# Two attention layers on one core: the output products of step 7 placed behind the value products, with the next scores after them

## The chip, the cores and the metric

The kernel runs on one core of a Trainium2 chip. The metric is the device time in microseconds: 3507.43 us before the change, the median of three runs (3504.42 to 3509.01). The profiled execution has a span of 3507.0 us, and the mean granted TensorE clock in it is 0.998.

## The reference

Four images of 32 x 32 positions with 768 channels pass through two layers. Each layer normalizes in 32 groups of channels, computes attention with 12 heads of 64 channels over the 1024 positions of the image, with a bias for relative height and width, projects the result, and adds it to its input. Cut to what matters:

```python
for Wq, Wk, Wv, Wproj, bproj, Rh, Rw in layers:      # layer 1 also has biases for q, k, v and scales twice
    n = group_norm(x)                                # 32 groups
    q, k, v = n @ Wq, n @ Wk, n @ Wv                 # 12 heads of 64
    s = scale * q @ k.T + (q @ Rh)[..., :, None] + (q @ Rw)[..., None, :]
    x = x + (softmax(s) @ v) @ Wproj + bproj
```

Everything is in float32.

## The kernel before

Activations lie with the channels on the 128 partitions and the 1024 positions (S) along the free axis. Two layers by four images make 8 image passes, run one after the other. Heads are worked in pairs: a pair is 128 channels, one head in partitions 0 to 63 and one in 64 to 127, six pairs (NP) to an image, 48 pairs (NPAIR) in all, counted by g. Each pair has 8 steps (NT), counted by n; a step is 128 query positions against all 1024 key positions, for both heads. The main loop at L566 goes through these 384 units (g, n) in order.

The order of the instructions is written out by hand: the block at L542 fixes it for all engines, and each engine runs its own instructions in the order in which the code issues them. The tile pools still add the waits for data and buffers. In one turn of the loop, unit (g, n), the code issues, in this order:

- run(early) at L595: what earlier steps left to be done, such as stores, loads of weights, the position products (L281) and the statistics for the next normalization (L152).
- biases (L319, GpSimd): the bias tile of the unit two ahead, 128 x 1024 for each head, into the pool sc.
- scores (L333) of the unit one ahead: eight TensorE instructions in four calls, into the PSUM pool ps_s, which has two buffers, one for each head. VectorE then adds the bias and finds the row extreme in one pass from PSUM to SBUF (L342, one for each head); this is what frees the PSUM buffer. ScalarE takes the exponential with the row sum (L346).
- run(behind) at L601: DMA reads that bring the transposed weights back.
- turn (L370, VectorE): the 32 x 32 block transposes of the weights of the unit itself, one for each head; every second step a DMA writes them to DRAM (td) and a later one reads them back (pt), which finishes the transposition.
- divide (L353 on VectorE, L356 on GpSimd): the reciprocals of the row sums of the unit one ahead, and the product of its exponentials with them.
- take: a share of a list of TensorE work that fills the step. The list of a pair is 36 parts for the next pair's projections (q and k at L214, v at L249), then 12 parts of output products (L475). The shares are 6, 6, 0, 6, 12, 6, 0, 12 by step, so that step 7 has the 12 output parts: four groups of three calls of 128 x 128 by 128 x 512, each evicted by VectorE (L486 or L488). The projections and the output products, like the value products, use the PSUM pool ps_m with two buffers.
- weigh (L399): the value products, for the first half of the queries at the end of step 6, for the second half at the end of step 2 of the next pair.

The output products of step 7 belong to an earlier image or to the pairs before, never to the weights just computed. In the first image, pairs 0 to 2 have none: there is no image before. In pair 4, three steps and step 7 also apply the next image's normalization on VectorE (L193), one pass for each of six chunks.

In TensorE's order, the border between two pairs is therefore: value products of step 6, scores of (g+1, 0), in step 7 the twelve output parts, then in step 0 of the next pair the scores of (g+1, 1) and the first six projection parts. Line numbers here and in the profile are those of the kernel before.

## Time and profile before

| engine | busy us | share of the span |
|---|---|---|
| PE (TensorE, matmuls) | 3462.3 | 99% |
| POOL (GpSimd) | 2729.9 | 78% |
| DVE (VectorE) | 2381.1 | 68% |
| PEld (weight loads) | 1921.4 | 55% |
| ACT (ScalarE) | 1227.5 | 35% |

DMA moves 1084.54 MB at a mean of 309 GB/s; in most slices of the span the 16 engines are 80 to 90% busy.

TensorE's busy time by kind of product: q and k projections 1033.5 us, scores 750.1, value products 689.1, v projections 515.7, output products 475.8 and 33.5 (those with the last weights), positions 108.7. These overlap, since products in different halves of the array run side by side, so their sum is above the engine's own busy time.

Each row of the groups by line gives the line, engine, operation, tiles written and read, shapes and the count; then the busy time and the mean length of one in ns; then the engine's idle time just before, and what ended most of it. In a timeline a row is a merged stretch: start, length, line, tiles, count, and in brackets the idle time before it with its cause. The ends of matmuls are modelled, so on TensorE the distance between starts says more than the lengths do.

### The profile page before, as it was taken

What the parts mean: (1) busy time and instruction counts of PE and PEld (TensorE: products, weight loads), DVE (VectorE), ACT (ScalarE), POOL (GpSimd) and SP (SyncE); (2) the same over time, 40 slices, a digit from 0 to 9 for tenths busy, and PEclk for the clock granted to TensorE, in tenths of its full rate; (3) what the DMA queues carried; (4) which work ended last, traced back from release to release, by engine and by line L of the source; (5) the groups of instructions that cost most, each with busy time, mean ns of one, the idle gap of its engine ahead of it and who ended that gap; (6) DMA issues with size and microseconds to landing.
All of it is one profiled execution on the core that took longest, in us unless ns stands there. A gap on an engine that the chain in (4) does not pass through costs nothing.

```text
span 3507.0 us, 55102 instructions
## 1 busy us (share of the span) xinstructions
PE 3462.3 (99%) x21120; PEld 1921.4 (55%) x21120; DVE 2381.1 (68%) x3676; ACT 1227.5 (35%) x2040; POOL 2729.9 (78%) x1546
## 2 busy tenths in 40 slices
PE   6999999999999999999999999999999999999999
PEld 4555555555555555555555555555555555555554
DVE  4666767767677676767767667666666667666666
ACT  2334333333333333333333333333333333333331
POOL 3888887778777787788777788787787778787774
PEclk9999999999999999999999999999999999999999
DMA  4889989999899898898989989899889988898877
GB/s 137 312 308 311 332 293 337 319 316 326 304 329 323 313 316 313 312 324 305 326 305 326 320 292 332 311 331 306 300 327 324 321 298 316 319 322 295 311 275 281
DMA packets 624857, 1084.54 MB, mean 309 GB/s; under 512 B 247120, under 2 KB 310096, under 8 KB 575440
## 3 DMA queue, kind: packets, MB, share of 16 engines
q1 hardware_dynamic: 569008, 1028.29, 83.4%
q10 hardware_dynamic: 55584, 52.72, 4.4%
q8 instruction: 166, 2.72, 0.3%
q14 instruction: 99, 0.81, 0.1%
HBM read 580.59 MB, written 500.27 MB: 308 GB/s over the span
## 4 chain that ended last, share of the span: by engine, by line
PE 97%; DMA 2%; DVE 0%; SPq 0%; issue 0%; ACT 0%; POOL 0%; ACTq 0%; DVEq 0%
PE pj L214 28%; PE s L333 19%; PE av L399 19%; PE o L475 14%; PE pv L249 14%; PE tp L281 3%; DMA tdr<-t 1%; DMA pt<-td 1%; SPq L307 0%; DMA td<-tb 0%; DMA wo<-in_wo 0%; DMA xn<-in_x 0%; DVE st L152 0%; DMA rel<-tdr 0%; DMA per<-mv 0%
## 5 line engine op out<-in xcount | busy, mean ns | idle before, releaser
L319 POOL TENSOR_TENSOR sc<-rel 128x1024 f32<-128x1024 f32 x768 | 1890.4, 2485 | 38.2 <-DMA rel<-tdr 38.2
L356 POOL TENSOR_SCALAR sc<-sc,sm 128x1024 f32<-128x1024 f32 x768 | 855.1, 1127 | 686.1 <-DVE sm L353 669.2
L346 ACT ACTIVATE sc<-sc,sm 128x1024 f32<-128x1024 f32 x768 | 879.8, 1147 | 1370.9 <-DVE sm L342 1368.7
L342 DVE CUSTOM_DVE_ANT_0 sc<-s,sc 128x1024 f32<-128x1024 f32 x768 | 909.8, 1222 | 293.3 <-PE s L333 266.4
L214 PE MATMUL pj<-xn,w 64*128 64x512 f32 x4608 | 1033.5, 591 | 26.8 <-DVE xn L193 25.7
L370 DVE STREAM_TRANSPOSE tb<-sc 128x1024 f32<-128x1024 f32 x768 | 910.7, 1222 | 22.9 <-DMA td<-tb 20.5
L214 PEld LDWEIGHTS pj<-xn,w 64*128 64x128 f32 x4608 | 453.2, 188 | 568.6 <-issue 536.6
L333 PE MATMUL s<-k,q 64*128 64x512 f32 x3072 | 750.1, 598 | 7.0 <-DVE sm L342 6.9
L399 PE MATMUL av<-pt,v 128*64 128x256 f32 x6144 | 689.1, 382 | 6.1 <-DMA pt<-td 6.1
L399 PEld LDWEIGHTS av<-pt,v 128*64 128x64 f32 x6144 | 434.5, 137 | 289.8 <-ACT v L259 35.6
L249 PE MATMUL pv<-wv,xn 64*128 64x256 f32 x4608 | 515.7, 376 | 0.0
L249 PEld LDWEIGHTS pv<-wv,xn 64*128 64x128 f32 x4608 | 448.3, 187 | 90.8 <-issue 30.1
L475 PE MATMUL o<-attn,wo 128*128 128x512 f32 x1080 | 475.8, 597 | 0.2 <-DMA wo<-in_wo 0.2
L333 PEld LDWEIGHTS s<-k,q 64*128 64x128 f32 x3072 | 288.5, 187 | 299.5 <-issue 275.5
L475 PEld LDWEIGHTS o<-attn,wo 128*128 128x128 f32 x1080 | 201.4, 190 | 271.4 <-issue 260.9
L260 DVE TENSOR_TENSOR v<-pv,v 128x256 f32<-128x256 f32 x192 | 81.5, 425 | 277.6 <-ACT v L259 277.6
L259 ACT COPY v<-pv 128x256 f32<-128x256 f32 x192 | 71.5, 372 | 330.7 <-PE pv L249 282.9
L286 ACT COPY t<-tp 128x1024 f32<-128x1024 f32 x96 | 97.2, 1012 | 245.5 <-PE tp L281 148.5
L346 ACT ACTIVATION_READ_ACCUMULATOR sc<-sc,sm 128x1 f32 x768 | 143.6, 187 | 0.0
L230 DVE TENSOR_TENSOR q<-pj,q 128x512 f32<-128x512 f32 x96 | 66.4, 692 | 107.5 <-ACT q L227 56.0
L230 DVE TENSOR_TENSOR k<-pj,k 128x512 f32<-128x512 f32 x96 | 66.4, 692 | 95.5 <-ACT k L227 49.0
L281 PEld LDWEIGHTS tp<-tab,q 64*128 64x128 f32 x1536 | 100.0, 187 | 39.9 <-issue 39.6
(34 smaller groups left out, 787.6 us busy)
## 6 DMA issues: line engine op xcount, KB each, us to landing
td<-tb SPq DMA_DIRECT2D x384, 1024.0 KB, 5.9
pt<-td SPq DMA_DIRECT2D x382, 1024.0 KB, 7.6
tdr<-t ACTq DMA_DIRECT2D x96, 512.0 KB, 6.3
w<-in_wqk SPq DMA_DIRECT2D x96, 384.0 KB, 7.5
rel<-tdr SPq DMA_DIRECT2D x760, 32.0 KB, 2.3
part<-res SPq DMA_DIRECT2D x84, 256.0 KB, 5.5
res<-part SPq DMA_DIRECT2D x84, 256.0 KB, 9.1
wv<-in_wv SPq DMA_DIRECT2D x24, 768.0 KB, 8.7
```

The lines of the kernel that those rows point to most:

```text
L214: nc.tensor.matmul(t[:, a, :], lhsT=w[rows, c, :], rhs=xn[c][rows, cols], start=(c == 0), stop=(c == NC - 1),)
L230: nc.vector.tensor_tensor(to, t[1], to, ALU.add)
L249: nc.tensor.matmul(t[:, a, k, :], lhsT=xn[c][rows, (2 * i + k) * P : (2 * i + k + 1) * P], rhs=w[rows, c, :], start=(c == 0), stop=(c == N ...
L281: nc.tensor.matmul(ps[:, h, j, :], lhsT=q[rows, at * P : (at + 1) * P], rhs=tabs[l][rows, :], start=True, stop=True,)
L319: nc.gpsimd.tensor_tensor(sc.rearrange("p (a k) (u l) -> p a (k u) l", a=4, l=8), rel[:, h, 0, n, :].unsqueeze(1).unsqueeze(3).to_broadcas ...
L333: nc.tensor.matmul(ps[h][:, cols], lhsT=q[rows, n * P : (n + 1) * P], rhs=k[rows, cols], start=True, stop=True,)
L342: nc.vector.tensor_tensor_reduce(out=sc, in0=ps[h], in1=sc, scale=-scale, scalar=BIG, op0=ALU.add, op1=ALU.min, accum_out=st[:, 0, h : h + 1],
L346: nc.scalar.activation(sc, sc, AF.Exp, bias=st[:, 0, h : h + 1], scale=-1.0, accum_out=st[:, 1, h : h + 1],)
L356: nc.gpsimd.tensor_scalar(sc, sc, st[:, 2, h : h + 1], 1.0, ALU.mult, ALU.mult)
L370: nc.vector.transpose(tb[:, :, j, :], sc_of[g, n, h])
L399: nc.tensor.matmul(av[rows, at * 2 * P : (at + 1) * 2 * P], lhsT=v_of[g][:, k, rows], rhs=pt_of[g, quarter, h][:, :, k, :], start=(k == 0) ...
L475: nc.tensor.matmul(t, lhsT=wo_of[im, o, c], rhs=attn_of[im * NP + c][:, cols], start=(c == c0), stop=(c == c1 - 1),)
```

## The change

In step 7, the transposes of the unit itself and the twelve output parts move ahead of the next scores. TensorE's order at the border becomes: value products of step 6, output products, scores of (g+1, 0), scores of (g+1, 1). Value and output products both use all 128 rows of the array, scores and projections 64, so the rows change from 128 to 64 once at the border, where they changed to 64, to 128 and to 64 again before.

In the other steps, scores and run(behind) change places in the code; one issues DMA on another queue, so each engine's own order stays. In pair 4, the normalizations of chunks 3 to 5 stand one behind each of the first three groups of output products; before, two of them stood together. VectorE's order in step 7 was: L342 for both heads, first eviction, transposes, reciprocal, remaining evictions. It becomes: transposes, four evictions, L342 for both heads, reciprocal.

```diff
             if at + 2 < len(units):
                 biases(*units[at + 2])
+            run(behind)
+            behind, behind2 = behind2, behind
+            share = shares[n]
+            if n == NT - 1:
+                turn(g, n)
+                if pair == 4 and not end:
+                    for c in (3, 4, 5):
+                        take(todo, 3)
+                        share -= 3
+                        apply(c)
+                take(todo, share)
+                share = 0
             if at + 1 < len(units):
                 scores(*units[at + 1])
-            run(behind)
-            behind, behind2 = behind2, behind
             if pair == 3 and n in stages and not end:
                 stages[n]()
             if pair == 4 and n in (2, 4, 6) and not end:
                 apply(n // 2 - 1)
-            share = shares[n]
-            first = 3 if n == NT - 1 else 2 if end and pair == NP - 1 and n in (3, 4) else 0
-            first = min(first, share)
+            first = min(share, 2 if end and pair == NP - 1 and n in (3, 4) else 0)
             take(todo, first)
             share -= first
-            turn(g, n)
+            if n < NT - 1:
+                turn(g, n)
             if at + 1 < len(units):
                 divide(*units[at + 1])
-            if pair == 4 and n == 7 and not end:
-                for chunks in ((3, 4), (5,)):
-                    take(todo, 3)
-                    share -= 3
-                    for c in chunks:
-                        apply(c)
             take(todo, share)
```

## The prediction

> **What bounds the kernel now.** I began with the busy shares and the chain that ended last, then the groups by line, then the tensor engine's timeline around steps 6, 7 and 0, and last the granted clock in short windows.

> ```profile
> PE 3462.3 (99%) x21120; PEld 1921.4 (55%) x21120; DVE 2381.1 (68%) x3676; ACT 1227.5 (35%) x2040; POOL 2729.9 (78%) x1546
> PE 97%; DMA 2%; DVE 0%; SPq 0%; issue 0%; ACT 0%; POOL 0%; ACTq 0%; DVEq 0%
> L333 PE MATMUL s<-k,q 64*128 64x512 f32 x3072 | 750.1, 598 | 7.0 <-DVE sm L342 6.9
> L370 DVE STREAM_TRANSPOSE tb<-sc 128x1024 f32<-128x1024 f32 x768 | 910.7, 1222 | 22.9 <-DMA td<-tb 20.5
> L356 POOL TENSOR_SCALAR sc<-sc,sm 128x1024 f32<-128x1024 f32 x768 | 855.1, 1127 | 686.1 <-DVE sm L353 669.2
> ```

> TensorE is the chain: 97% of it, and scores wait only 6.9 us for VectorE in the whole run. VectorE and GpSimd have slack (GpSimd idles 686 us before L356). So the order of products on TensorE, and what they wait for, decides. The ordinary border between two pairs, in the timeline (start, length, line, tiles, count):

> ```profile
> 319.69 3.19 PE L399 MATMUL av<-pt,v 128*64 128x256 f32 x28
> 322.81 1.99 PE L333 MATMUL s<-k,q 64*128 64x512 f32 x8
> 324.73 10.57 PE L475 MATMUL o<-attn,wo 128*128 128x512 f32 x24
> 335.23 1.99 PE L333 MATMUL s<-k,q 64*128 64x512 f32 x8
> 337.05 5.32 PE L214 MATMUL pj<-xn,w 64*128 64x512 f32 x24
> ...
> 351.77 0.44 PE L399 MATMUL av<-pt,v 128*64 128x256 f32 x2
> ```

> Value products av, scores of (g+1, 0), output products o, scores of (g+1, 1), with no gap. The output products stand between two sets of scores. In image 0, pairs 0 to 2 have no output products in step 7 (there is no earlier image), so the border from pair 2 to pair 3 already has the two sets of scores adjacent, as the change makes it everywhere:

> ```profile
> 258.98 1.99 PE L333 MATMUL s<-k,q 64*128 64x512 f32 x8
> 262.39 2.70 PE L333 MATMUL s<-k,q 64*128 64x512 f32 x7 [1.43 <-DVE sm L342]
> 264.51 0.59 PE L214 MATMUL pj<-xn,w 64*128 64x512 f32 x1
> ...
> 280.08 1.30 PE L399 MATMUL av<-pt,v 128*64 128x256 f32 x10
> ```

> The second set waits for VectorE, because the score pool has two buffers, one per head, and both hold the first set until L342 has read them. VectorE at that place:

> ```profile
> 261.11 1.22 DVE L342 CUSTOM_DVE_ANT_0 sc<-s,sc 128x1024 f32<-128x1024 f32 x1 [0.45 <-PE s L333]
> 262.26 1.22 DVE L342 CUSTOM_DVE_ANT_0 sc<-s,sc 128x1024 f32<-128x1024 f32 x1
> 263.40 2.37 DVE L370 STREAM_TRANSPOSE tb<-sc 128x1024 f32<-128x1024 f32 x2
> ```

> At the border before that one (scores at 127.94) the clock dropped as well. In the granted clock of short windows (length, PE busy with count, clock, DMA share, GB/s):

> ```profile
> 133.00:133.50 0.50, 0.50 (x4) 0.67 1.05 393
> 133.50:136.50 3.00, 3.00 (x10) 0.50 1.08 420
> 136.50:137.00 0.50, 0.50 (x6) 0.92 0.85 360
> ```

> [...] half clock lasts from 133.17 to 136.58 (3.41 us) and again from 198.02 to 201.44, and the two onsets are 64.85 us = 19 x 3.413 apart. [...] Here av is 128x64, o 128x128, scores and projections 64x128; scores at 342.20 hand over to same-mode products after 1.72 us, those before an o after 1.92 us, so a switch costs about 0.2.

> **The change, part by part.**
> (a) Which borders: 47 borders between pairs, less the three of image 0 that are adjacent already (pairs 0, 1, 2): 44. In the last pair nothing follows.
> (b) One border before, from the start of the value products of step 6 to those of the next step 2: av 7.06 (1749.65 to 1756.71 in a later border), scores to o 1.92 (322.81 to 324.73), o 10.50 (to 335.23), then 16.54 (to 351.77). Sum 36.02.
> (c) The same after: av 7.06, since av handing over to o is in the trace too, at the end (3462.87 to 3469.93, 7.06; the first thing that I had hoped to save is not there). o to scores 10.50, unchanged. Then the adjacent scores, as from 258.98 to 280.08: 21.10. Sum 38.66. Difference +2.64 us a border. It already contains what is saved by one mode switch less.
> (d) The same from VectorE's side: L342 starts 2.13 us after the scores do and takes 1.15 us to the next one, so the buffer of head 1 is free at 4.4, and its second scores start 4.56 after the first instead of at 1.72: 2.84 late. The 0.2 of the saved switch off gives the 2.64. Head 0 starts at 3.41, but the projections behind need both halves of the array, so head 1 sets the end.
> (e) Half clock. The border with scores at 193.47 has the wait and a half-clock window: 193.47 to the value products at 216.24 is 22.77, and 127.94 to 150.74 is 22.80; against 21.10 that is +1.67 to 1.70, half of 3.41. How often? Counted from the start of the first scores, the window ahead of the drop began at +1.14 (198.02 - 3.41 - 193.47) and at +1.82 (133.17). At 258.98 a window began at +0.48, and at the very first adjacent pair (57.5) at +0.58: no drop. So windows that begin at +1.14 to +1.82 drop, those at +0.5 don't; the edge is between, at about +0.9. A period before is 71.70 us (41 pairs from 324.7 to 3264.2 in 2939.5); after, 74.34 without a drop, which is 0.76 short of 22 windows (75.09): the next window begins 0.76 later on its border. With a drop, 76.01: 0.92 earlier, as 76.01 is 0.92 over 22 windows. The phase climbs by 0.76 until it is in the zone of about one us and is thrown back by 0.92, so it hardly jumps over. Balance: 0.76 / (0.76 + 0.92) = 0.45 of the borders. 0.45 x 44 = 20 drops x 1.67 = 33 us.
> (f) The transposes of step 7 move ahead of the output products, and the three normalizations of pair 4 between them, all on VectorE: 2.37 us of transposes ready at about av's end (GpSimd's division before ends at 1757.1, o starts at 1756.9 in the changed order), then four evictions of 0.75. The third o needs the first one's buffer 5.2 us after the o's start, VectorE gives it after some 3.7. No cost: the 10.5 us of o hides it. The last eviction ends under 1 us after the scores start (with the statistics of layer 0, 0.68 + 0.21, by about 1.75), before L342's 2.13.
> (g) The reciprocal of (g+1, 0) now follows L342 directly and waits on VectorE for both exponentials (two of 1.15 us behind L342), up to about 6.2 us after the first scores. Queued behind it is L342 of (g+1, 1), whose scores end at 6.3 at the earliest; GpSimd's divisions wait for it too. At 258.98 that L342 began at 6.75 and cost nothing more. GpSimd then has 7.1 us of work a step against 6.9 to 12 of TensorE and had idle time; it catches up in step 4. No cost.
> Sum: 44 x 2.64 = 116, and 33: 3507.4 + 149 = 3657.

> **The rivals.**
> Rival A, no half clock: the o products ahead keep the array busy, or the phase misses. Against it: two of the four adjacent score pairs of this trace dropped, and those had full activity ahead as well. 3507.4 + 116 = 3624.
> Rival B, nearly every border drops: the zone is wider than I put it, or the phase locks inside. Nothing forbids it, the two undropped cases lie within 0.1 us of each other in phase. 44 x (2.64 + 1.67) = 190: 3697.
> Rival C, faster: the scores aren't held, and one mode switch less a border is all that remains, 44 x 0.2 = 9, hence 3498. It would need L342 to run ahead; the 1.43 us wait on L342 at three borders speaks against.

> **How the numbers follow.** The forecast (a third to six tenths of the borders at half clock) 0.62, A and rare drops 0.17, B 0.14, C 0.03, and 0.04 for something near 3507 or beyond 3697. The range starts a little under A, 3620, takes in the forecast and most of the way to B, 3690. Faster by over 0.2%: 0.03; within: 0.02; slower: 0.95.

> **What would show it.** In the changed profile: scores waiting on L342 at each border, 47 or so times 1.4 us, instead of 6 times; the mean granted clock down, with 20 windows of 3.41 us at half, 68 us of 3657, so about 0.99; the evictions and transposes without waits on TensorE; the period of a pair between 74.3 and 76.0. Step (c) is wrong if the second scores start under 3 us after the first; (e) if the count of half-clock windows is near 0 or 44; (f) if the output products wait for VectorE. Slower than 3697 would mean that GpSimd's late division holds something in steps 0 to 3.

## The result, and the profile after

The changed kernel takes 3668.43 us (median of four runs, 3667.74 to 3668.62) against 3506.48 us of the kernel before in the same set of runs: a ratio of 1.0461, with a 95% interval of 1.0443 to 1.0479. It is slower by 162 us. The profiled execution has a span of 3666.0 us, 159.0 more than before, and a mean granted TensorE clock of 0.986.

The busy shares, the chain and the groups by line of the changed kernel:

```profile
PE 3556.7 (97%) x21120; PEld 1985.7 (54%) x21120; DVE 2385.3 (65%) x3676; ACT 1229.5 (34%) x2040; POOL 2720.2 (74%) x1546
PE 95%; DMA 2%; DVE 1%; issue 1%; SPq 0%; ACT 0%; POOL 0%; ACTq 0%; POOLq 0%
L333 PE MATMUL s<-k,q 64*128 64x512 f32 x3072 | 879.5, 614 | 71.1 <-DVE sm L342 70.1
```

TensorE is still the chain. The same 3072 score instructions are busy for 879.5 us in place of 750.1, and wait 70.1 us for VectorE in place of 6.9. The wait shows only part of the loss: a score set that has one head's buffer and waits for the other's counts as busy (at the border below, one stretch of 2.70 us for the second set against 1.99 for the first), and so does a product at half clock (3.00 of 3.00 us busy at a clock of 0.52, below). So I read the rest from distances between starts.

A border without a drop of the clock, on the changed kernel's TensorE timeline:

```profile
1901.76 7.13 PE L399 MATMUL av<-pt,v 128*64 128x256 f32 x64
1908.82 10.57 PE L475 MATMUL o<-attn,wo 128*128 128x512 f32 x24
1919.32 1.99 PE L333 MATMUL s<-k,q 64*128 64x512 f32 x8
1922.62 2.70 PE L333 MATMUL s<-k,q 64*128 64x512 f32 x7 [1.32 <-DVE sm L342]
1924.74 0.59 PE L214 MATMUL pj<-xn,w 64*128 64x512 f32 x1
...
1940.31 1.95 PE L399 MATMUL av<-pt,v 128*64 128x256 f32 x16
```

From the value products of step 6 to those of step 2 it takes 1940.31 - 1901.76 = 38.55 us, where the kernel before took 36.02. The border ahead of it ran through a drop, that is, one window of 3.41 us at half clock (granted clock in short stretches; length, PE busy with count, clock, DMA share, GB/s):

```profile
1848.00:1848.50 0.50, 0.50 (x4) 1.00 0.80 266
1848.50:1851.50 3.00, 3.00 (x10) 0.52 1.05 405
```

There, 1825.84 to 1866.08 is 40.24 us. Of the 44 borders, 22 take 38.5 and 22 take 40.2 us, nearly always in turn. 22 x 2.52 + 22 x 4.22 = 148 us. The three borders of image 0 account for most of what remains of the 159: the time from the start of the run to the fourth pair's value products of step 6 grew from 315.75 to 324.45, by 8.7 us. That part I had not forecast. One of these borders in the changed kernel:

```profile
263.23 1.99 PE L333 MATMUL s<-k,q 64*128 64x512 f32 x8
268.32 4.07 PE L333 MATMUL s<-k,q 64*128 64x512 f32 x7 [3.10 <-DVE sm L342]
...
288.77 7.13 PE L399 MATMUL av<-pt,v 128*64 128x256 f32 x64
```

From the first scores to the value products, 25.54 us against 21.10 before. At each of the three borders half clock now lasts 6.83 us, two windows; before it was one window at two of them and none at the third. At 1.70 us a window, these four more make 6.8 of the 10 us by which the three stretches grew together; the rest is longer waiting. And VectorE at the first of these borders (scores at 126.69):

```profile
128.25 2.32 DVE L370 STREAM_TRANSPOSE tb<-sc 128x1024 f32<-128x1024 f32 x2
130.49 1.19 DVE L342 CUSTOM_DVE_ANT_0 sc<-s,sc 128x1024 f32<-128x1024 f32 x1
```

The transposes now stand ahead of L342, and here no output products hide them: L342 starts 3.80 us after the scores, not 2.13.

### The profile page after: what moved, and what is told of

It is laid out like the page before. It is cut to its first block, busy times and chain, and to the rows that moved or that the text cites. A ratio compares the mean times of both kernels' runs of the same rounds, so it can differ in the third digit from the quotient of the medians.

```text
span 3666.0 us, 55145 instructions
## 1 busy us (share of the span) xinstructions
PE 3556.7 (97%) x21120; PEld 1985.7 (54%) x21120; DVE 2385.3 (65%) x3676; ACT 1229.5 (34%) x2040; POOL 2720.2 (74%) x1546
## 4 chain that ended last, share of the span: by engine, by line
PE 95%; DMA 2%; DVE 1%; issue 1%; SPq 0%; ACT 0%; POOL 0%; ACTq 0%; POOLq 0%
PE pj L214 27%; PE s L333 21%; PE av L399 18%; PE o L475 13%; PE pv L249 13%; PE tp L281 3%; DMA tdr<-t 1%; DVE sc L342 1%; DMA pt<-td 1%; DMA td<-tb 0%; DVE tb L370 0%; SPq L307 0%; DVE st L152 0%; DMA xn<-in_x 0%; DMA rel<-tdr 0%
## 5 line engine op out<-in xcount | busy, mean ns | idle before, releaser
L356 POOL TENSOR_SCALAR sc<-sc,sm 128x1024 f32<-128x1024 f32 x768 | 854.1, 1128 | 854.0 <-DVE sm L353 841.4
L214 PE MATMUL pj<-xn,w 64*128 64x512 f32 x4608 | 1135.5, 601 | 26.5 <-DVE xn L193 25.4
L342 DVE CUSTOM_DVE_ANT_0 sc<-s,sc 128x1024 f32<-128x1024 f32 x768 | 911.2, 1222 | 231.1 <-PE s L333 195.8
L333 PE MATMUL s<-k,q 64*128 64x512 f32 x3072 | 879.5, 614 | 71.1 <-DVE sm L342 70.1
L370 DVE STREAM_TRANSPOSE tb<-sc 128x1024 f32<-128x1024 f32 x768 | 908.9, 1221 | 10.7 <-DMA td<-tb 10.2
L214 PEld LDWEIGHTS pj<-xn,w 64*128 64x128 f32 x4608 | 509.0, 193 | 575.4 <-issue 537.1
L399 PE MATMUL av<-pt,v 128*64 128x256 f32 x6144 | 689.1, 382 | 7.1 <-DMA pt<-td 7.1
L399 PEld LDWEIGHTS av<-pt,v 128*64 128x64 f32 x6144 | 434.6, 137 | 290.7 <-ACT v L259 35.6
L333 PEld LDWEIGHTS s<-k,q 64*128 64x128 f32 x3072 | 344.9, 189 | 414.3 <-issue 240.0
L475 PE MATMUL o<-attn,wo 128*128 128x512 f32 x1080 | 475.8, 597 | 0.0
L475 PEld LDWEIGHTS o<-attn,wo 128*128 128x128 f32 x1080 | 201.4, 190 | 254.7 <-issue 247.6
L281 PEld LDWEIGHTS tp<-tab,q 64*128 64x128 f32 x1536 | 124.6, 187 | 31.0 <-issue 29.6
L281 PE MATMUL tp<-tab,q 64*128 64x128 f32 x1536 | 134.4, 281 | 0.0
```

The lines of the kernel that those rows point to most:

```text
L214: nc.tensor.matmul(t[:, a, :], lhsT=w[rows, c, :], rhs=xn[c][rows, cols], start=(c == 0), stop=(c == NC - 1),)
L281: nc.tensor.matmul(ps[:, h, j, :], lhsT=q[rows, at * P : (at + 1) * P], rhs=tabs[l][rows, :], start=True, stop=True,)
L333: nc.tensor.matmul(ps[h][:, cols], lhsT=q[rows, n * P : (n + 1) * P], rhs=k[rows, cols], start=True, stop=True,)
L342: nc.vector.tensor_tensor_reduce(out=sc, in0=ps[h], in1=sc, scale=-scale, scalar=BIG, op0=ALU.add, op1=ALU.min, accum_out=st[:, 0, h : h + 1],
L356: nc.gpsimd.tensor_scalar(sc, sc, st[:, 2, h : h + 1], 1.0, ALU.mult, ALU.mult)
L370: nc.vector.transpose(tb[:, :, j, :], sc_of[g, n, h])
```

## The experiments

My theory: the second set of scores waits for the two PSUM buffers that VectorE has not yet read (2.5 us a border), and the pause lets the clock drop when the border meets the clock's windows at a certain phase. The rivals: the order itself costs (output products behind value products, mode switches); the reciprocal and the division that come late on VectorE and GpSimd cost; the drops belong to the order and not to the pause.

### Four buffers for the two sets

In the changed kernel, the scores of steps 0 and 1 take one of their two buffers each from the projections' pool.

```diff
-        ps = [ps_s.tile([P, S], FP, tag="s", name=f"s_{g}_{n}_{h}") for h in range(2)]
+        ps = [
+            (ps_m if n == h else ps_s).tile([P, S], FP, tag="m" if n == h else "s", name=f"s_{g}_{n}_{h}")
+            for h in range(2)
+        ]
```

> The changed order, with one difference: the scores of step 0 take a buffer of the projections' PSUM pool for head 0, those of step 1 for head 1, so the two adjacent sets have four buffers in place of two. Theory (the second set waits only for the buffers that VectorE has not read yet): no wait and no half clock at any border, 36.02 us before becomes about 35.8 (one mode switch less, about 0.2 to 0.3), and the stalls of the first three borders (12 us in the kernel before) go too: 3506 - 10 - 12, so 3480 to 3490, faster than both kernels. Rival (the order itself costs: output products directly behind value products, or the division and reciprocal that come late on GpSimd and VectorE): stays near 3660. Rival (half clock comes from the order and not from the wait): about 3545.

Measured: 3529.01 us against 3507.82, ratio 1.0062 (1.0047 to 1.0077). The total misses the forecast of 3480 to 3490 by some 40 us, but the border is just as forecast. On TensorE's timeline (L478, L336 and L402 are the former L475, L333 and L399):

```profile
1764.72 10.57 PE L478 MATMUL o<-attn,wo 128*128 128x512 f32 x24
1775.22 3.70 PE L336 MATMUL s<-k,q 64*128 64x512 f32 x16
1778.75 5.32 PE L214 MATMUL pj<-xn,w 64*128 64x512 f32 x24
```

Both sets run as one stretch of 16 without a pause, and the border takes 35.82 us: 2.7 less than in the changed kernel, 0.20 less than before. TensorE's order is that of the changed kernel, instruction by instruction, so neither that order nor a late division costs at the border; the 0.20 fits one mode switch less, which the prediction put at about 0.2. Some 7 us are lost in the first pair, where projections wait up to 6.2 us for the borrowed buffers and the clock stands at half for 10.2 us. More, 26 us in the profiled run, is lost in pair 4 of six of the seven images that have a next one, where the stretch from the value products of step 2 to those of step 6 took 38.4 to 40.4 us in place of 35.68 (five of the six with a window at half clock). The rest of the miss stays open. VectorE, GpSimd and TensorE at one of these, from their timelines:

```profile
355.03 6.38 DVE L193 TENSOR_SCALAR xn<-xn,nrm 128x1024 f32<-128x1024 f32 x1
356.00 4.87 POOL L319 TENSOR_TENSOR sc<-rel 128x1024 f32<-128x1024 f32 x2
364.38 7.12 PE L214 MATMUL pj<-xn,w 64*128 64x512 f32 x24 [2.48 <-DVE attn L411]
```

A normalization takes 6.38 us where one without GpSimd beside it takes 0.80, and ends at 361.41, 0.54 us after GpSimd's biases end at 360.87. The eviction of the value products queues behind it, and TensorE waits 2.48 us for that. The changed kernel shows the same on a smaller scale: its 14 normalizations in pair 4 with nothing of GpSimd beside them take 0.80 us each, and the 14 longest, of 2.43 to 4.60 us, end 0.54 to 0.56 us after biases do. What holds them up is not shown. GpSimd had been idle at the border for 11.05 us, waiting for the late reciprocal, and then ran without a pause in steps 0 to 2, so that the normalization of step 2 found no gap.

### Three projection parts between the sets

```diff
+            if n == 0:
+                take(todo, 3)
+                share -= 3
             if at + 1 < len(units):
                 scores(*units[at + 1])
```

> The changed order, with three of step 0's six projection parts (2.57 us) moved between the two sets of scores. Theory: the second scores would come at 1.8 + 2.57 = 4.4 us and head 1's buffer is there at 4.56, so at most 0.3 us is left of the stall and no half clock; border 36.0 to 36.1 us, and in image 0 the stalls shrink from 12 to about 6 us: 3498 to 3510. Rival (late division or the order of output products): near 3660. It also tells the mode switch: what it is under 36.02 + 0.2 is saved by one switch less.

Measured: 3523.76 us against 3507.82, ratio 1.0053 (1.0036 to 1.0069). The border is 36.07 us, within the forecast, and none of the 44 has a drop of the clock. The total lies above the forecast of 3498 to 3510, and most of that stands in the same place as above: steps 3 to 6 of pair 4 take up to 39.95 us in five images, 16 us together.

### One part between the sets

The same edit with 1 in place of 3.

> The changed order with one of step 0's projection parts (0.86 us) between the two sets of scores. Theory: the wait shrinks by 0.86 us, from 2.53 to 1.67 net a border, and TensorE is active in more of each window, so that the half-clock windows at the 44 borders go altogether: 3507 + 44 x 1.67 + some 5 to 9 of image 0, 3580 to 3592. Rival (drops belong to the adjacency or the order, not to the activity in a window): 22 x 1.69 = 37 us more, 3617 to 3629.

Measured: 3592.05 us against 3508.59, ratio 1.0235 (1.0220 to 1.0250). The total is at the upper end of the forecast. The border is 37.68 us at all 44 (37.69 at some), 1.66 above the kernel before where 1.67 was forecast, and no window at half clock falls on any of them. One of them:

```profile
1950.62 1.99 PE L333 MATMUL s<-k,q 64*128 64x512 f32 x8
1952.44 1.02 PE L214 MATMUL pj<-xn,w 64*128 64x512 f32 x4
1953.93 2.70 PE L333 MATMUL s<-k,q 64*128 64x512 f32 x7 [0.46 <-DVE sm L342]
```

The window in which the pause lies began, in steps of 3.413 us, at 1952.00, 1.38 us after these first scores. The next one, where a drop would show:

```profile
1955.42:1958.83 3.41, 3.41 (x18) 1.00 1.00 350
```

A lucky phase is ruled out as well: over the 44 borders a window begins anywhere from 0.1 to 3.1 us after the first scores, at 13 of them within 1.04 to 1.86, where every one dropped in the changed kernel, and none drops here. So one part between the sets took 0.86 us off every border (38 us) and all 22 drops away (37 us), together nearly all of the 76 us to the changed kernel, although 1.66 us of stall stay. A pause of 0.46 us, as in this timeline, brings no drop, one of 1.32, as in the changed kernel, brings 22 at 44 borders: neither the order nor a wait as such makes them.

### The padding

If the drops follow from the phase between the borders and the clock's windows, then more work in a pair should shift them. In the changed kernel, the first product of the first output group at each border is done twice; the second overwrites the first.

```diff
         for c in range(c0, c1):
+            if c == c0 and (2 * o + i) % 4 == 0 and (p == 0 or not end):
+                nc.tensor.matmul(
+                    t, lhsT=wo_of[im, o, c], rhs=attn_of[im * NP + c][:, cols],
+                    start=True, stop=True,
+                )
             nc.tensor.matmul(
```

> The changed kernel, with the first output product of the first group at each border done twice (the second overwrites the first): 0.875 us more TensorE work a pair, 45 times, 39 us in all. Theory (drops of the clock are set by the phase between the border and a free-running window of 3.413 us): a pair without a drop then takes 74.22 + 0.88 = 75.10 us, which is 22 windows, so the phase stands still; at the third pair's border it is 1.3 us (a drop), the drop throws it to 3.0, outside the zone of 1.0 to 1.9, and there it stays: 1 half-clock window or none in place of 22 after image 0, 36 us back for 39 us of work: 3668 to 3675. Rival (every second border drops by something else that repeats, as image transfers or buffers do): 3668 + 39 = 3707. Rival (more work in the stretch costs the same as everywhere, drops at random): 3700 to 3715.

> The kernel before with the same extra product: the cost of the padding by itself. Theory: TensorE is the chain and has no slack, so 45 x 0.875 = 39 us: 3545 to 3548. Rival (it fits in a gap): 3507.

> The changed kernel with half of that extra product (256 of 512 columns, 0.44 us a pair, 20 us in all). Theory (phase against the free-running window): a pair without a drop takes 74.66 us, 0.43 short of 22 windows, one with a drop 76.35, 1.26 over; so 0.43 / 1.69 = a quarter of the 44 borders drop, about 11, and the mean pair stays at 75.09 us: the time is again that of the changed kernel, 3666 to 3672. Rival (drops alternate as before, whatever the length of the pair): 22 drops and 3688.

| kernel | time, us | border without, with drop, us | borders with a drop |
|---|---|---|---|
| changed | 3668.43 | 38.54, 40.24 | 22 |
| changed, half padding | 3668.04 (3665.97 to 3671.96) | 38.98, 40.67 | 11 |
| changed, padding | 3667.43 (3665.31 to 3669.62) | 39.40, - | 0 |
| before | 3506.48 | 36.02, - | 0 |
| before, padding | 3550.36 (3546.96 to 3553.26) | 36.88, - | 0 |

The mean granted clock and the span of the changed kernel, of the padded and of the half-padded one, in this order:

```profile
core 0: 3666.0 us, clock 0.986
```
```profile
core 0: 3664.3 us, clock 0.997
```
```profile
core 0: 3665.6 us, clock 0.992
```

In the kernel before, the extra product costs 0.86 us a pair and the run takes 42 us more than the kernel before in its own set of runs (3508.59), a little above the forecast of 3545 to 3548. In the changed kernel the same 39 us of work cost nothing, because as much time at half clock goes away (22 drops of 1.70 us). The count of drops is the forecast one in both (0 or 1, and 11), though with the full padding the phase did not stand still where I had put it: the windows began at first 0.3 us after the scores, not 3.0, which lies outside the zone too. The three times are alike because in all three a pair takes 22 windows (75.09 us) on average, as near as the starts tell: 74.22 and 75.92 in turn (mean 75.07); three of 74.66 to one of 76.35 (75.08); 75.08 each. In these kernels, in which the pair without a drop is up to 0.87 us shorter than 22 windows, the drops make up the difference. The rivals on alternation (3688 to 3707) fall.

### The transposes

Only the transposes of step 7 ahead of the next L342, with TensorE's order of before:

```diff
+            if n == NT - 1:
+                turn(g, n)
             if at + 1 < len(units):
                 scores(*units[at + 1])
```

> The kernel before, with only the transposes of step 7 moved ahead of the next scores' VectorE work; TensorE's order is that of before. Theory: at the 44 borders with output products nothing changes, as 10.5 us of products stand between the scores. At the first three borders VectorE reads the scores about 1.7 us later and the half-clock stretch gets longer: the three took 66.7 us before and 76.6 in the changed kernel, so +9 us: 3513 to 3517. Rival (the first three borders got longer by the order of something else): 3506. Rival (early transposes delay the evictions or scores everywhere): 3520 or more.

Measured: 3518.4 us against 3507.82, ratio 1.0028 (1.0017 to 1.0038), so 6 to 13 us more, a little above the forecast of 3513 to 3517. The 44 borders stay at 36.02 us. TensorE's waits on L342, in the kernel before and in this one (us in total, times, longest):

```profile
PE s L333 <- DVE sm L342: 6.9, 6, 1.4
```
```profile
PE s L333 <- DVE sm L342: 11.9, 6, 3.1
```

Six waits as before, but up to 3.1 us long. How much that costs varies between executions, and the other profiles tell: up to the fourth pair's value products of step 6, this kernel and both padded versions of the changed one give each engine the same work in the same order as the changed kernel. These products start at 321.20, 324.80 and 323.58 us, against 324.45 in the changed kernel. With late transposes they start at 315.75 in the kernel before, at 314.91 in its padded version and at 313.93 in the kernel described next. So the early transposes are what the first borders paid for, 8.6 us from mean to mean.

The other half, the changed kernel with the transposes behind the scores again:

```diff
-            if n == NT - 1:
-                turn(g, n)
...
-            if n < NT - 1:
-                turn(g, n)
+            turn(g, n)
```

> The changed kernel with the transposes of step 7 back behind the next scores' VectorE work; output products stay ahead of the scores. Theory: the 44 borders stay at 38.5 without and 40.2 us with half clock, the first three return to what they were before, -9 us: 3658 to 3662. Rival (the early transposes share in the cost of all borders): 3630 or less. Rival (they hid under the output products what now lies behind the scores): above 3668.

Measured: 3857.56 us, ratio 1.1013 (1.0951 to 1.1076): 190 us slower than the changed kernel, where I had forecast 9 faster. The third expectation holds in direction, at a size that none had. The transposes' row in the groups by line, of the changed kernel and of this one:

```profile
L370 DVE STREAM_TRANSPOSE tb<-sc 128x1024 f32<-128x1024 f32 x768 | 908.9, 1221 | 10.7 <-DMA td<-tb 10.2
```
```profile
L370 DVE STREAM_TRANSPOSE tb<-sc 128x1024 f32<-128x1024 f32 x768 | 919.3, 1226 | 380.9 <-DMA td<-tb 378.4
```

The transposes of step 7 then come a step's output products later, and their write-outs with them. From there on VectorE waits 378 us for write-outs to free the three transpose buffers, their median time to land goes from 6.1 to 8.6 us, and TensorE waits 85.3 us for weights to be read back (37 times) in place of 7.1. With the scores behind the output products, the early transposes are needed. How much is the late start and how much the crowding of the queue wasn't separated.

### A version that beats both

Four buffers again (not in the first pair), with the normalizations of pair 4 moved away from GpSimd's busy stretch, and early transposes only where output products hide them.

```diff
-            if pair == 4 and n in (2, 4, 6) and not end:
-                apply(n // 2 - 1)
+            if pair == 4 and n in (5, 6) and not end:
+                apply(n - 5)
...
-                    for c in (3, 4, 5):
+                    for c in (2, 3, 4, 5):
...
+            late = n < NT - 1 or not todo
...
-                turn(g, n)
+                if not late:
+                    turn(g, n)
...
-            if n < NT - 1:
+            if late:
                 turn(g, n)
```

> The four score buffers at the border again (not in the first pair), with two further edits: the normalizations of pair 4 moved from steps 2, 4, 6 to steps 5 and 6 and the four last of them between the output products of step 7, where GpSimd is idle; and the early transposes only where there are output products. Theory (in the four-buffer kernel GpSimd runs without a pause in steps 0 to 4 of a pair, and a normalization on VectorE waits for it up to 6.4 us, which holds TensorE in pair 4): the losses of 2.5 to 4.7 us in pair 4 go, border 35.8 us: 3483 to 3492. Rival (the losses in pair 4 come from the buffers borrowed from the projections): 3510 to 3530.

Measured: 3497.06 us against 3508.59, ratio 0.9968 (0.9959 to 0.9977): faster than both kernels, though 5 us above the range I had put. Steps 3 to 6 of pair 4 are back at 35.68 us while the buffers are still borrowed, so the rival falls. The normalization's row, of the four-buffer kernel and of this one:

```profile
L193 DVE TENSOR_SCALAR xn<-xn,nrm 128x1024 f32<-128x1024 f32 x48 | 99.6, 2084 | 3.5 <-DMA nrm<-back 3.5
```
```profile
L193 DVE TENSOR_SCALAR xn<-xn,nrm 128x1024 f32<-128x1024 f32 x48 | 49.2, 1034 | 3.4 <-DMA nrm<-back 3.4
```

What is missing: the fourth pair's first value products wait for a read-back (about 5 us in the profiled run), and the last border, where step 0 of the last pair has output products that need the borrowed buffers, takes 39.85 us.

## Why the prediction was right

The forecast was 3657, slower; measured 3668.4, within the range and 11 us above the number.

- **(a) to (d), the wait.** The difference at a border without half clock was put at 2.64 us and is 2.52. It is smaller by 0.12, nearly all of it because L342 starts 2.02 us after scores that follow output products, not 2.13. That the wait lies in the buffers is shown by the four-buffer kernel: with them the border falls from 38.54 to 35.82 us in the same order.
- **(c), the mode switch.** That av hands over to o at the same price as to scores held: 7.06 us. The 0.2 for the switch saved fits too, 36.02 against 35.82.
- **(e), half clock.** Put at 20 drops of 1.67 us; there were 22 of 1.70, at the 44 borders. Counted from the first scores as the prediction did, the windows ahead of a drop began at +1.02 to +1.86 and those without a drop at +0.22 to +0.99, so the edge lies at 1.0 where I had put 0.9. That a fixed step of 3.413 us runs through the whole trace was an estimate from two onsets 64.85 us apart; the 28 onsets of the changed kernel bear it out. That the phase against it decides is shown by both paddings, with 11 drops and with none in place of 22. The phase also explains why a wait that was put too long and drops that were counted too few cancel: the balance in (e) amounts to a mean pair of 22 windows, so the 44 pairs grow by 44 x (75.09 - 71.70) = 149 us with the forecast numbers and with the measured ones; the borders gave 148.
- **(f), the transposes.** "No cost: the 10.5 us of o hides it" holds for the 44 borders and is where the prediction fell short: I counted out the first three borders in (a) as adjacent already, and did not ask what the early transposes do where nothing hides them. They cost 8.7 us, most of the 11. Nor had I seen that moving them was needed: left behind the scores, they cost 190 us.
- **(g), the late reciprocal.** TensorE's own borders show no cost of it (35.82 with four buffers). But GpSimd's catching up does cost once the wait on TensorE is gone: a normalization in pair 4 then stands beside GpSimd's work and takes 6.4 us. In the changed kernel itself the same normalization takes 2.9 us, and 4.6 in two images, but the steps keep to 35.68 us (35.97 in those two), so the term was right there but for 0.6 us.
- **The rivals.** A (no half clock) and B (nearly all) both missed the count; C fell with the first border.

## What to carry to other kernels

Before two producers are put side by side, count the buffers that the second one needs and who empties them: what stood between them was hiding the consumer, not only filling the time (here 10.5 us of output products, and without them a wait of 1.32). A move that is hidden at most places has to be priced at those where the hiding work is missing, as at the first passes of a loop. And a pause that is short against everything else can go with a drop of the clock, as 1.32 us in a pair of 74.22 did at 22 of 44 borders, so a small change of length can cost nothing (39 us of padding) or pay twice (one part between the sets: 38 us of wait and 37 of half clock); read the period against the spacing of the drops, here 3.413 us, before trusting a difference of one or two per cent.

## What the runs showed of the hardware

A window ahead of half clock need not be idle: in the changed kernel, the 22 windows ahead of a drop at the borders began 1.02 to 1.86 us after the first scores, and TensorE was busy for 2.07 to 2.08 of their 3.41 us. The 22 at the other borders, which began at 0.22 to 0.99 us, were busy for 2.09 to 2.10 us and had full clock behind them. The profile's busy time rests on modelled ends, so I estimate from the starts, at 0.43 us from one product to the next (1.72 us for the four of a head in a set), that a window at the edge, which begins 1.0 us after the first scores, holds 0.7 us of the first set and 0.9 us of one head of the second: products in some 1.6 us of the 3.41. The kernel with such a pause locked to a whole number of windows: 39 us more work on TensorE left the run at 3667 us, with the mean clock up from 0.986 to 0.997, and the mean pair at 75.08 us, 22 windows. And a normalization of 0.80 us on VectorE took 6.38 us beside GpSimd's biases, ending 0.54 us after them.
